# One-core attention and mixture-of-experts kernel: the next image's Layer 0 from turn 12 on, sorting in every other turn beside expert tiles, and a reordered tail

## The chip, the cores and the metric

The kernel runs on one core of one Trainium2 chip, as one program in one launch. Its time is the device time of a whole execution in microseconds; the median of several executions is compared. Everything is float32.

## The reference

The input x has 8 images of 256 channels by 32x32 pixels, that is 1024 tokens of 256 values each. Three stages follow each other for every image, and images do not mix.

```python
# Layer 0: deformable attention with a learned position bias
x = x + L0(_gn(x))          # L0: q = wq x; a 6x6 depthwise convolution (stride 4), gelu, 1x1, tanh -> 64 offsets;
                            # sample x there -> k, v (64 keys); for each query and key an MLP of the signed-log
                            # distance gives the bias: relu(relu(pos w1) w2) w3;  softmax(q k + bias) v ; w_out
# Layer 1a: sigmoid attention over the 1024 tokens of the image
t = t + sigmoid(LN(t) qw LN(t)^T) LN(t)
# Layer 1b: mixture of experts, top 2 of 8
t = t + moe(LN(t))          # moe: u + sum over the two chosen e of weight_e * (gelu(u w1[e]) w2[e] + b2[e])
```

The position bias is the bulk of the work: for each image a two-layer network of width 64 over 1024 queries x 64 keys x 4 heads.

## The kernel before

**The turn.** The program is unrolled. Its main loop runs 8 images x 64 turns (`for n in range(NB * TURNS)`, `b, i = divmod(n, TURNS)`). Each turn makes two tiles of the bias network. `first_layer` writes one tile `h` on DVE (L463) and one on POOL (L465), two turns ahead of use. `second_layer` multiplies two tiles on PE (`h2p`, L478) and rectifies one on ACT (L484) and one on DVE (L486). In even turns `third_layer` adds four finished tiles to the logits (`sim`, L505). The PSUM pool of `h2p` has two buffers, so the second product of a turn cannot start before L486 of the turn before has emptied its buffer.

**What is laid beside it.** All other work is written as Python generators, and each turn advances some of them by one step, so that the order on every engine is the order of the calls. At the end `in_order` fixes it: every engine carries out its instructions in the order in which the program issued them. In one turn the calls come in this order: the bias tiles, `side.step()`, `advance(mains)`, `mix(b, i)`, `step(sums)`.

- `side` holds the softmaxes of the logits (`waiting`) and `prep`, Layer 0 of the next image: statistics, normalization, two projections (`qs`, L272), the 36 taps of the convolution on DVE (L284, L286, three a step), gelu, the offset projection (`op`, L297), tanh, positions (`gk`, `ft`), sampling weights `wt` (ACT L377 and L379, POOL L368), transposes (`tp`, L374), and keys and values (`kv` L386, `kp`, `kd`).
- `mains` holds `attention`, in two halves. `upper` runs in turns 53 to 63 of its own image, `rest` in the next image's turns 0 and on: `to_query` (5 to 11), the attention `slots` (12 to 28), the normalization `finish` (to 33), the sort `route`, and 16 indirect DMAs on POOL (L775) that send the tokens to the rows of their experts in DRAM.
- `route` is six steps on DVE with little else: two picks of the best expert, running counts, the count product `cnt` on PE (L842), the slots (`slot`), and which expert owns each tile (`which`, `expert`). It keeps the one bank of the PSUM pool `acc` from its first step to its last. `cnt` is taken in its fourth step and read to the end in the fifth, in one of the two buffers of the pool `psum`.
- `mixtures` holds `experts` of the image two before: 12 tiles of 256 rows (15 single-expert tiles for the last image). One step stores tile n-2 (`yp` L921, `yt` L926, `ys`), computes tile n-1 (`hp` L939, `ht` L947), and loads and transposes tile n (`xl` L900, `tp` L957, `xg` L959). Weights are fetched through SP, with the expert's number read from `expert` (L906, L907).
- `sums` holds `combine` of the image three before: gathers `gs` on POOL (L992), a weighted sum on DVE (`xc`, L984), transposes and stores.

While `attending` is set, `aside` takes its bank from `psum`, else from `acc`. While `sorting` is set, `side` starts no softmax step and no step of `prep`. So in the loop the sort stands alone in turns 34 to 39, the sends follow in turns 40 to 55, and `mix` has no tile due in turns 35, 37 and 39. Image 0 has no `rest`, images 0 and 1 have no tiles, and image 7 has no `prep`.

**The tail.** After the loop, `rest` of the last image goes on, with one step of `mixtures` (image 6) after every second step until the sort has begun, and after every step from there on. Then the last image's experts and sums alternate.

Of the kernel before, what the change touches and what calls it, by code (L numbers as in the profile page):

```python
# [16 lines left out]
P = 128  # L17
# [86 lines left out]
def tile_conv_attn_hybrid(ctx: ExitStack, tc: tile.TileContext, x, par, qw, w1, w2_, cst, out):  # L104
# [32 lines left out]


    attending = sorting = False

    def aside(name):
        return psum(name) if attending else acc(name)
# [72 lines left out]
    def run(steps):  # L215
        for _ in steps:
            pass
# [374 lines left out]


    def attention(b, st, o, rt):
        nonlocal attending
        x = xres.pop(b)
        x1, tt, tn, qt = None, None, None, None

# [148 lines left out]
        def rest():  # L747
            nonlocal attending, sorting, ut, lqs
            for n, _ in enumerate(softmax(st, 1, 1, st["last"], o, psum)):
                if n == 1:  # L750
                    residual_bias(1)
                yield
            yield from to_query(1)
            ut = tokens("ut")
            lqs = low("lqs", (P, Q))
            attending = True

            for n, _ in enumerate(slots([(q, mp) for q in range(4) for mp in range(2 if q < 2 else 0, 4)], True)):
                if n % 3 == 0:
                    yield  # L760
                    others()
                yield
                others()
            attending = False
            while finishing:
                yield
                others()
            attending = sorting = True
            yield from route(lqs, rt, LARGE if b == NB - 1 else SMALL)
            attending = sorting = False  # L770

            xs, group = xss[b % 2], f"slots{b}"
            for n in range(16):
                m, c = divmod(n, 2)
                sent = nc.gpsimd.indirect_dma_start(  # L775
                    out=xs[:, :], out_offset=bass.IndirectOffsetOnAxis(ap=rt["slot"][:, c, m : m + 1], axis=0),
                    in_=ut[:, m, :], in_offset=None,
                )
                if n:
                    tc.declare_no_dep(sent.ins, group=group, reason="other slots")  # L780
                tc.add_to_no_dep_group(group, sent.ins)
                sents.add(sent.ins.name)
                yield
            rt.update(xs=xs, xu=xu)
            mixtures.append((b, experts(b, rt)))
# [6 lines left out]
    def route(lqs, rt, slots_):  # L792
# [74 lines left out]
            nc.vector.tensor_reduce(place[:, c], part(1), AX.X, ALU.add)  # L867
        slot = held("slot", (P, 2, 8), I32)
        nc.vector.tensor_copy(slot, place)  # L869
        yield  # L870
        which = bank[:, 0 : TILES * (E - 1)].rearrange("p (t e) -> p t e", e=E - 1)
        nc.vector.tensor_tensor(
            which, ends[:, 1:8].unsqueeze(1).to_broadcast([P, TILES, E - 1]),
            cst_("tiles").unsqueeze(2).to_broadcast([P, TILES, E - 1]), ALU.is_le,
# [2 lines left out]
        nc.vector.tensor_reduce(whose, which, AX.X, ALU.add)  # L877
        expert = held("expert", (P, TILES), I32)
        nc.vector.tensor_copy(expert, whose)
        yield  # L880
        rt.update(slot=slot, expert=expert, w=ws)

# [1 line left out]
    def experts(b, rt):  # L886
        xs = rt["xs"]
        slots_ = LARGE if b == NB - 1 else SMALL

        several = LARGE // slots_  # L890
        rounds = -(-tiles_of(slots_) // several)
        yv = dram.tile([rounds * LARGE, C], F32, name=f"ys{slots_}")
        rows, tokens_, first, second = {}, {}, {}, {}

        def at(t):
            return slice(t * LARGE, (t + 1) * LARGE)

        def fetch(t):
            rows[t] = low("xl")
            nc.sync.dma_start(out=rows[t], in_=xs[at(t), :].rearrange("(s p) c -> p s c", p=P))  # L900

        def weights(t, pool, width, w, name):
            f = pool.tile([P, 2, width], F32, name=name)
            for u in range(several):
                n = t * several + u
                e = nc.sync.value_load(rt["expert"][0:1, n : n + 1], min_val=0, max_val=E - 1)  # L906
                nc.sync.dma_start(out=f[:, u, :], in_=w[bass.ds(e, 1)].rearrange("e p c -> (e p) c"))  # L907
            return f

        fetch(0)  # L910
        yield
        fetch(1)
        first[0] = weights(0, w1pool, 2 * C + 2, w1, "w1")
        yield
        for n in range(rounds + 2):
            if n >= 2:
                f2, ht = second.pop(n - 2), tokens_.pop(n - 2)
                yp = psum("yp").rearrange("p (s c) -> p s c", s=2)
                for s in range(2):
                    for f in range(2):  # L920
                        nc.tensor.matmul(  # L921
                            yp[:, s, :], lhsT=ht[:, f, s * P : (s + 1) * P],
                            rhs=f2[:, s * several // 2, f * C : (f + 1) * C], start=(f == 0), stop=(f == 1),
                        )
                yt = low("yt")
                nc.vector.tensor_tensor(yt, yp, f2[:, 0:several, 2 * C :].to_broadcast([P, 2, C]), ALU.add)  # L926
                nc.sync.dma_start(out=yv[at(n - 2), :].rearrange("(s p) c -> p s c", p=P), in_=yt)
            if n + 2 < rounds:
                fetch(n + 2)
            if n < rounds:  # L930
                second[n] = weights(n, w2pool, 3 * C, w2_, "w2")
            if 1 <= n <= rounds:
                f1, xg = first.pop(n - 1), tokens_[n - 1]
                hp = psum("hp").rearrange("p (f i) -> p f i", f=2)
                for f in range(2):
                    for u in range(several):
                        us = slice(u * slots_, (u + 1) * slots_)
                        for k in range(2):
                            nc.tensor.matmul(  # L939
                                hp[:, f, us], lhsT=f1[:, u, k * C + f * P : k * C + (f + 1) * P], rhs=xg[:, k, us],  # L940
                                start=(k == 0), stop=(k == 1),
                            )
                tokens_[n - 1] = ht = low("ht")
                for f in range(2):
                    for u in range(several):
                        us = slice(u * slots_, (u + 1) * slots_)
                        nc.scalar.activation(  # L947
                            ht[:, f, us], hp[:, f, us], AF.Gelu, bias=f1[:, u, 2 * C + f : 2 * C + f + 1]
                        )
            if n + 1 < rounds:  # L950
                first[n + 1] = weights(n + 1, w1pool, 2 * C + 2, w1, "w1")
            if n < rounds:
                xl = rows.pop(n)
                tp = aside("tp").rearrange("p (k i) -> p k i", k=2)
                for k in range(2):
                    for s in range(2):
                        nc.tensor.transpose(tp[:, k, s * P : (s + 1) * P], xl[:, s, k * P : (k + 1) * P], ident)  # L957
                tokens_[n] = xg = low("xg")
                nc.scalar.copy(xg, tp)  # L959
            if n < rounds + 1:  # L960
                yield
        sums.append((b, combine(b, rt, yv)))
# [35 lines left out]
    class Side:  # L998
# [2 lines left out]
        def __init__(self, prep_steps):  # L1001
            self.prep, self.waiting, self.busy, self.left = prep_steps, [], True, True

        def step(self):
            busy = False
            if self.waiting and not (sorting and self.busy):
                busy = self.busy
                self.busy = next(self.waiting[0], None)
                if self.busy is None:
                    self.waiting.pop(0)  # L1010
                    self.busy = True
            if self.left and not busy and not sorting:
                self.left = next(self.prep, self) is not self

        def finish(self):
# [49 lines left out]
    def mix(b, i):  # L1065
        of = mixtures[0][0] if mixtures else NB
        if of == b - 2 and b < NB - 1:
            due = i in (24, 26) or i > 26 and i % 2 and i not in (35, 37, 39, 59, 61, 63)
        elif of == b - 3:
            due = i == 9  # L1070
        else:
            due = b == NB - 1 and (i >= TURNS - 2 if of == b - 1 else of < b and i > 9 and (i % 2 or i % 3 == 0))
        if due:
            step(mixtures)
# [4 lines left out]

    for n in range(NB * TURNS):  # L1080
        b, i = divmod(n, TURNS)
        if i == 0:
            steps = iter(())
            if b + 1 < NB:
                xb = big("xb")
                nc.sync.dma_start(out=xb, in_=xin(b + 1))
                steps = prep(b + 1, xb, sts[b + 1])
            side = Side(steps)
# [21 lines left out]
        if coming_ < total:  # L1110
            if n % 8 == 3:
                scale()
            elif n % 8 == 4:
                second()
        if i > 4:
            side.step()
        if ready:
            side.waiting.append(ready)
        if i == 0 and b:
# [11 lines left out]
    n = sorted_ = 0  # L1131
    while mains:
        advance(mains)
        if sorted_ or not attending and n % 2:
            step(mixtures)
        sorted_ = sorted_ or sorting
        n += 1
    while mixtures:
        step(mixtures)
# [111 lines left out]
```

## Time and profile before

| what | value |
|---|---|
| median of 3 runs | 3132.17 us (3131.75 to 3134.66) |
| the profiled execution, its own time | 3125.55 us |
| its span, first to last instruction | 3123.8 us |
| PE busy | 2832.1 us (91%), mean granted clock 0.975 |
| DVE busy | 2170.5 us (69%) |
| ACT, POOL busy | 1824.4 us (58%), 1558.2 us (50%) |
| main loop (turn 0 of image 0 to turn 63 of image 7) | 72.9 to 2867.0 us |
| one image in the loop, images 2 to 6 | 358.3, 363.8, 362.3, 364.5, 362.4 us |

The start of a turn is told by the ACT instruction of `second_layer` (L484), of which there is one in each turn; the 512 of them cut the span into turns of 2.4 to 12 us. Idle time of PE inside a turn is what that turn has lost, as long as PE has the most work there. Where DVE has more, PE's idle time shows DVE's excess. The profiled execution is 6.6 us shorter than the median of the runs.

### The profile page before, as it was taken

What the parts mean: (1) busy time and instruction counts of PE and PEld (TensorE: products, weight loads), DVE (VectorE), ACT (ScalarE), POOL (GpSimd) and SP (SyncE); (2) the same over time, 40 slices, a digit from 0 to 9 for tenths busy, and PEclk for the clock granted to TensorE, in tenths of its full rate; (3) what the DMA queues carried; (4) which work ended last, traced back from release to release, by engine and by line L of the source; (5) the groups of instructions that cost most, each with busy time, mean ns of one, the idle gap of its engine ahead of it and who ended that gap; (6) DMA issues with size and microseconds to landing.
All of it is one profiled execution on the core that took longest, in us unless ns stands there. A gap on an engine that the chain in (4) does not pass through costs nothing. (4 is left out here: it accounts for less than half of the span.)

```text
span 3123.8 us, 51635 instructions
## 1 busy us (share of the span) xinstructions
PE 2832.1 (91%) x19592; PEld 1395.6 (45%) x19592; DVE 2170.5 (69%) x2999; ACT 1824.4 (58%) x2533; POOL 1558.2 (50%) x945
## 2 busy tenths in 40 slices
PE   3888998899999999999999999899999999979975
PEld 2223343233545344453545445354444545514764
DVE  4897678967776687857876678766877574595122
ACT  3666565665576566665566656665666666554322
POOL 2546454744455364645556455553646443383122
PEclk7999999999999999999999999999999999989998
DMA  3312101211256125531346223561245325631386
GB/s 106 83 32 48 21 14 32 58 38 21 75 139 187 23 63 140 168 107 43 77 111 208 51 57 100 144 179 33 61 132 173 88 78 153 173 97 57 112 280 221
DMA packets 428297, 311.21 MB, mean 100 GB/s; under 512 B 284432, under 2 KB 368656, under 8 KB 428048
## 3 DMA queue, kind: packets, MB, share of 16 engines
q1 hardware_dynamic: 415472, 273.14, 32.7%
q0 software_dynamic: 12288, 33.57, 3.4%
q8 instruction: 154, 2.52, 0.3%
q10 hardware_dynamic: 288, 1.20, 0.1%
q14 instruction: 95, 0.78, 0.1%
HBM read 239.93 MB, written 67.90 MB: 99 GB/s over the span
## 5 line engine op out<-in xcount | busy, mean ns | idle before, releaser
L465 POOL TENSOR_TENSOR h<-ta,nb 128x1024 f32<-128x1024 f32 x512 | 1071.6, 2095 | 1036.2 <-PE h2p L478 913.1
L478 PE MATMUL h2p<-h,pr__100 64*64 64x512 f32 x8192 | 1028.3, 610 | 131.8 <-DVE h L486 107.5
L486 DVE TENSOR_TENSOR h<-h2p,nc 128x1024 f32<-128x1024 f32 x512 | 624.6, 1220 | 461.4 <-PE h2p L478 454.7
L484 ACT ACTIVATE h<-h2p,pr__100 128x1024 f32<-128x1024 f32 x512 | 570.9, 1115 | 517.0 <-PE h2p L478 515.8
L463 DVE TENSOR_TENSOR h<-ta,nb 128x1024 f32<-128x1024 f32 x512 | 769.2, 1503 | 0.3
L470 ACT ACTIVATE h<-h 128x1024 f32<-128x1024 f32 x512 | 538.0, 1051 | 63.4 <-POOL h L465 63.2
L478 PEld LDWEIGHTS h2p<-h,pr__100 64*64 64x64 f32 x8192 | 253.7, 133 | 658.0 <-issue 295.1
L505 PE MATMUL sim<-h,pr__100 128*32 128x512 f32 x4096 | 511.5, 618 | 0.0
L505 PEld LDWEIGHTS sim<-h,pr__100 128*32 128x32 f32 x4096 | 109.5, 112 | 377.8 <-issue 377.8
L713 PE MATMUL ap<-qt,tn 128*128 128x256 f32 x1024 | 250.5, 388 | 0.5 <-ACT nc L451 0.5
L727 PE MATMUL vp<-tt,sg 128*128 128x256 f32 x1024 | 243.3, 381 | 0.3 <-ACT sg L718 0.3
L992 POOL DMA_INDIRECT gs<-ys,slot x128 | 139.0, 1086 | 175.3 <-DMA ys<-yt 55.7
L713 PEld LDWEIGHTS ap<-qt,tn 128*128 128x128 f32 x1024 | 185.2, 190 | 88.5 <-issue 55.0
L947 ACT ACTIVATE ht<-hp,w 128x128 f32<-128x128 f32 (+1 forms) x366 | 108.6, 377 | 196.8 <-PE hp L939 173.2
L921 PE MATMUL yp<-w,ht 128*128 128x256 f32 x792 | 196.2, 390 | 13.7 <-DMA w<-in_w 7.0
L727 PEld LDWEIGHTS vp<-tt,sg 128*128 128x128 f32 x1024 | 193.2, 190 | 33.2 <-issue 6.9
L939 PE MATMUL hp<-xg,w 128*128 128x128 f32 (+1 forms) x1464 | 197.0, 287 | 6.7 <-ACT gk L307 2.8
L939 PEld LDWEIGHTS hp<-xg,w 128*128 128x128 f32 x1464 | 187.8, 194 | 18.3 <-ACT gk L307 3.7
L775 POOL DMA_INDIRECT xs<-ut,slot x128 | 167.8, 1311 | 51.0 <-DVE slot L869 29.4
L921 PEld LDWEIGHTS yp<-w,ht 128*128 128x128 f32 x792 | 144.4, 191 | 73.0 <-issue 34.0
L926 DVE TENSOR_TENSOR yt<-yp,w 128x512 f32<-128x512 f32 x99 | 68.3, 690 | 153.5 <-PE yp L921 127.3
L286 DVE SCALAR_TENSOR_TENSOR oc<-qp,pr__100,oc 128x128 f32<-128x128 f32 x280 | 168.9, 603 | 7.2
(266 smaller groups left out, 2468.0 us busy)
## 6 DMA issues: line engine op xcount, KB each, us to landing
w<-in_w SPq DMA_DIRECT2D x183, 384.0 KB, 3.6
w<-in_w SPq DMA_DIRECT2D x183, 257.0 KB, 3.7
ta<-fd SPq DMA_DIRECT2D x128, 256.0 KB, 5.5
xl<-xs SPq DMA_DIRECT2D x99, 256.0 KB, 3.7
ys<-yt SPq DMA_DIRECT2D x99, 256.0 KB, 2.3
nb<-fd SPq DMA_DIRECT2D x128, 128.0 KB, 5.3
xb<-in_x SPq DMA_DIRECT2D x8, 1024.0 KB, 7.2
x<-in_x SPq DMA_DIRECT2D x8, 1024.0 KB
```

Source lines behind the costliest of these rows:

```text
L286: nc.vector.scalar_tensor_tensor(oc, tap, dw[:, t : t + 1], oc, ALU.mult, ALU.add)
L463: nc.vector.tensor_tensor(h1, a, b, ALU.max)
L465: nc.gpsimd.tensor_tensor(h1, a, b, ALU.subtract)
L470: nc.scalar.activation(h1, h1, AF.Relu)
L478: nc.tensor.matmul(h2p[gs, r, :], lhsT=par_("w2")[rs, gs], rhs=h1[rs, g].rearrange("p y x -> p (y x)"), start=True, stop=True, tile_positi ...
L484: nc.scalar.activation(h2, h2p, AF.Relu, bias=par_("cb2"))
L486: nc.vector.tensor_tensor(h2.rearrange("p r (y x) -> p r y x", x=W), h2p.rearrange("p r (y x) -> p r y x", x=W), nc_.unsqueeze(3).to_broad ...
L505: nc.tensor.matmul(sim[32 * q : 32 * q + 32, :], lhsT=par_("z3")[:, 15 - m : 47 - m], rhs=h2s[2 * u + q // 2][:, q % 2, :], start=False, s ...
L713: nc.tensor.matmul(ap[:, u, :], lhsT=tn[:, k, m0 : m0 + P], rhs=qt[:, k, quarter(q)], start=(k == 0), stop=(k == 1),)
L727: nc.tensor.matmul(vp[:, i, :], lhsT=sg_[:, u, i * P : (i + 1) * P], rhs=tt[:, 2 * mp + u, :], start=(first and u == 0 and i == 0), stop=( ...
L921: nc.tensor.matmul(yp[:, s, :], lhsT=ht[:, f, s * P : (s + 1) * P], rhs=f2[:, s * several // 2, f * C : (f + 1) * C], start=(f == 0), stop ...
L939: nc.tensor.matmul(hp[:, f, us], lhsT=f1[:, u, k * C + f * P : k * C + (f + 1) * P], rhs=xg[:, k, us], start=(k == 0), stop=(k == 1),)
```

## The change

Four things move; no arithmetic is added or removed.

1. `prep` may start in turn 12 instead of turn 5 (image 0 excepted), and no longer stops for the sort.
2. In the loop, the first five steps of the sort are taken in odd turns only, 35 to 43. In the even turns between them `side` goes on; in the odd ones it doesn't. The sixth step (`which`, `expert`) moves behind the second send, in turn 45, and `which` is written to SBUF instead of to the PSUM bank. The sends fall in turns 44 to 59 instead of 40 to 55.
3. Tiles of `experts` are due in turns 24 and 26, and in the odd turns 31 to 55. Before they were due in 24 and 26, 27, 29, 31, 33, and in the odd turns 41 to 57. So each of the sort's five odd turns now holds a step of `experts` too.
4. In the tail, tiles come after every second step of the sort, not after each; and the first tile's `w1` is requested ahead of its tokens (everywhere, in the loop too).

```diff
@@ attention, rest
-            yield from route(lqs, rt, LARGE if b == NB - 1 else SMALL)
+
+            steps = route(lqs, rt, LARGE if b == NB - 1 else SMALL)
+            for _ in range(5):
+                while b < NB - 1 and turn % 2 == 0:
+                    yield
+                next(steps)
+                yield
             attending = sorting = False
...
                 sents.add(sent.ins.name)
+                if n == 1:
+                    run(steps)
                 yield
@@ route
         nc.vector.tensor_copy(slot, place)
-        yield
-        which = bank[:, 0 : TILES * (E - 1)].rearrange("p (t e) -> p t e", e=E - 1)
+        rt.update(slot=slot, w=ws)
+        yield
+        which = one.tile([P, TILES, E - 1], F32, name="which")
...
         nc.vector.tensor_copy(expert, whose)
-        yield
-        rt.update(slot=slot, expert=expert, w=ws)
+        rt.update(expert=expert)
@@ experts
+        first[0] = weights(0, w1pool, 2 * C + 2, w1, "w1")
         fetch(0)
         yield
         fetch(1)
-        first[0] = weights(0, w1pool, 2 * C + 2, w1, "w1")
         yield
@@ Side
-        def step(self):
+        def step(self, both=True):
...
-            if self.left and not busy and not sorting:
+            if self.left and both and not busy:
@@ mix
-            due = i in (24, 26) or i > 26 and i % 2 and i not in (35, 37, 39, 59, 61, 63)
+            due = i in (24, 26) or 30 < i < 56 and i % 2
@@ main loop
+        turn = i
...
-        if i > 4:
-            side.step()
+        if i > 4 and not (sorting and i % 2):
+            side.step(i > (11 if b else 4))
@@ tail
-        if sorted_ or not attending and n % 2:
+        sorted_ = sorted_ or sorting
+        if n % 2 if sorting else sorted_ or not attending and n % 2:
             step(mixtures)
-        sorted_ = sorted_ or sorting
```

What that does to the turns of an image with tiles (2 to 6), in the order of the program:

| work | turns before | turns after |
|---|---|---|
| `prep`: statistics and normalization | 5 to 11 | 12 to 20 |
| `prep`: `qs` projections | 12, 13 | 21, 22 |
| `prep`: 36 taps, three a step | 14 to 27 | 23 to 32, 34, 36 |
| `prep`: gelu, `op`, positions | 28 to 34 | 38 to 47 |
| `prep`: `wt`, `tp`, then `kv`, `kp` | 43 to 48, then 50, 52 | 50 to 56, then 57, 58 |
| sort, five steps | 34 to 38 | 35, 37, 39, 41, 43 |
| sort, sixth step | 39 | 45 |
| sends | 40 to 55 | 44 to 59 |

More of the change, by code (lines that the diff above doesn't have):

```diff
@@ L139, in tile_conv_attn_hybrid @@
     attending = sorting = False
+    turn = 0
     def aside(name):
@@ L594, in attention @@
     def attention(b, st, o, rt):
-        nonlocal attending
         x = xres.pop(b)
```

## The prediction

> **What bounds the kernel now.** I read the page first, then where PE waits within one steady image, then the stretches with idle time, then the instructions in them.
>
> ```profile
> span 3123.8 us, 51635 instructions
> PE 2832.1 (91%) x19592; PEld 1395.6 (45%) x19592; DVE 2170.5 (69%) x2999; ACT 1824.4 (58%) x2533; POOL 1558.2 (50%) x945
> PE   3888998899999999999999999899999999979975
> ```
>
> PE is the bound almost everywhere; only the start and the last slices are thin. A reordering can win idle time of PE and nothing else: about 280 us, of which 190 lie in the loop. Here are the longest waits of PE in image 4 (1404.1 to 1766.4 us):
>
> ```profile
> PE h2p L478 <- DVE h L486: 8.8, 7, 2.0
> PE q L649 <- ACT tn L642: 1.8, 1, 1.8
> ```
>
> Image 4 loses 16.9 us in all, and half of it is PE waiting for DVE to empty the PSUM buffer of the bias product. The busy times of stretches show where (first three rows: turns 6 to 8, 28 to 33 and 34 to 41 of image 4; last row: turns 28 to 49 of image 1, which has no expert tiles):
>
> ```profile
> core 0: us, PE busy (x) PEld busy (x) DVE busy (x) ACT busy (x) POOL busy (x), PEclk, DMA share, GB/s
> 1438.38:1450.74 12.36, 10.26 (x88) 2.70 (x84) 11.26 (x24) 6.17 (x7) 6.18 (x5) 1.00 0.08 12
> 1566.42:1601.82 35.40, 34.04 (x270) 18.59 (x266) 21.84 (x35) 25.35 (x43) 16.73 (x9) 1.00 0.53 133
> 1601.82:1639.77 37.95, 31.67 (x241) 10.74 (x237) 33.60 (x59) 22.99 (x29) 20.87 (x11) 0.96 0.31 78
> ...
> 505.33:609.50 104.17, 84.60 (x644) 24.73 (x640) 94.80 (x118) 66.82 (x86) 67.55 (x39) 0.95 0.21 48
> ```
>
> In rows 1, 3 and 4 DVE has more work than PE, and PE's idle time is that excess. In row 2 PE has far more. The third row is the sort: 6.3 us idle. One of its stalls in the timeline:
>
> ```profile
> 1608.31 2.63 DVE L463 TENSOR_TENSOR h<-ta,nb 128x1024 f32<-128x1024 f32 x1
> 1610.86 1.21 DVE L486 TENSOR_TENSOR h<-h2p,nc 128x1024 f32<-128x1024 f32 x1
> ...
> 1612.12 1.57 PE L478 MATMUL h2p<-h,pr__100 64*64 64x512 f32 x8 [1.97 <-DVE h L486]
> ```
>
> The sort's ops delay L463, L463 delays L486, and PE stands 1.97 us. L463 takes 1.22 us where nothing is in its way, here 2.63.
>
> [...] L463 (1.22 or 2.63 us) and the tap L286 (0.45 us in the timeline, 0.603 in the mean, up to 2.0) have two SBUF inputs, L486 reads PSUM and stays at 1.2. So a DVE-bound stretch is longer than its bare sums. [...] The trace has clock 0.96 in the sort's row; its 1.57 us for 8 products of L478, against 1.09 elsewhere, is such a phase. Image 5 has the same stalls without it and isn't shorter, so I give it no gain. [...] the request of `w1` goes out at 3015.19, behind the two fetches of tokens that waited until 3013.46.
>
> **The change, part by part.** PE's work is the same, so each part is idle time of PE, for one image of 2 to 6 unless said.
>
> *Prep leaves turns 5 to 11.* DVE loses four L243 (0.68 us), two L244 (0.21), and the small statistics (0.75 together), some 3.9 us in turns 5 to 7, PE two products (0.8). The 2.0 us stall of turn 8 goes: image 7, which has no prep, doesn't have it. The stall of 1.8 us at `q` stays: POOL's L465 stands there behind a gather that waits for the last `ys`, and that order is untouched. In turns 12 and 13 PE loses `qs` (4 us) while DVE gains the statistics; DVE then has 10.3 us for PE's 8.5, turns 11 and 14 are PE's and cover most: -0.2. Part: **+1.8**.
>
> *Tiles leave turns 27 to 33, taps enter.* PE loses two and a half tile steps (yp 1.99, hp 1.95, tp 0.60, so 4.5 us each) and gets fewer `op` products: 34.0 - 10 = 24 us. DVE loses two yt (0.69) and the position ops (3.0), and gains five groups of taps: at 0.603 us 9.0, so 21.8 - 4.4 + 9.0 = 26.5[...]. The row turns from PE-bound to DVE-bound. Following the L463, L486 and h2p of each turn from row to row I get stalls of 2 us in turns 31 and 32 and 4.0 in all. Bounds: bare taps at 0.45 leave 1.9[...]. The 1.36 us that PE loses in turn 29 today (waits for ACT there) go. Part: **-2.6** (-5.3 to -0.5).
>
> *Sort beside tiles.* The odd turns 35, 37, 39 get a tile step (4.5 us of PE) next to 1.4 to 2.4 us of sort on DVE, and turns 41 and 43 keep theirs. PE then has 6.5 to 8 us in an odd turn, DVE 5 to 6: the 6.3 us of turns 34 to 41 are covered. What is late next: in turn 41 `cnt` takes one of the two `psum` buffers until turn 43, and `attending` sends `tp` there too, so yp, hp and tp go through the other one by one. hp waits for yt (0.7 to 1.5 us), tp for four ht (1.14 us and a start). The tail shows such a step today (hp waited for yt, below). I take 2.5 us, and 1.0 for the softmax, `which` and yt that meet in turn 45: DVE has some 8 us there, PE 7 and a free turn after it. Sends, `wt` and L465 on POOL make 4.7 us of a turn of 6 to 8 in turns 53 to 56. Part: 6.3 - 3.5 = **+2.8** (0 to 4.5).
>
> Moved `kv`, `kp`, position ops: they lie in turns where PE has its own work, and the next image reads them in its turn 2, 44 turns' work of slack shrunk to 8. SP's nine small loads move from 34 to 47; the bias terms that read them are asked for in turn 56. `w1` ahead of the tokens in turn 24: the sends landed long before, nobody waits on SP. Each of these: nothing; if the cover were gone, the 2 us of one stall.
>
> Sum for an image of 2 to 6: +1.8 - 2.6 + 2.8 = +2.0; five images **+10**.
>
> *Image 1* is DVE-bound in turns 28 to 49 (94.8 of 104.2 us). Seven groups of taps enter (bare 9.4 us). PE's 5.5 us wait in turn 31 for the blocking chain gelu, tanh, log goes, since its steps now have a turn between them; so do 2 us of turn 8 and some 2 in turns 57 and 58, filled by `kv`. Net **-2** (-6 to +3). *Image 7*: same DVE sum, spread wider, DVE-bound still: 0. *Image 0*: untouched.
>
> *Tail.* Today:
>
> ```profile
> 2986.44 0.69 DVE L926 TENSOR_TENSOR yt<-yp,w 128x512 f32<-128x512 f32 x1 [2.26 <-PE yp L921]
> 2987.19 3.78 PE L939 MATMUL hp<-xg,w 128*128 128x128 f32 x16 [0.78 <-DVE yt L926]
> 2988.82 1.03 POOL L775 DMA_INDIRECT xs<-ut,slot  x1 [26.98 <-DVE slot L869]
> ...
> 3013.46 0.87 SPq L900 DMA_DIRECT2D xl<-xs  x2
> 3015.19 0.36 SPq L907 DMA_DIRECT2D w<-in_w  x1
> ```
>
> The sort lies 2972.6 to 2988.5 with three tiles in it. With one tile less ahead of the slots, they come some 6 us sooner, and the 16 sends (1.27 us apart) end at about 3003 in place of 3008.9. But the tokens can be fetched only behind the last `ys` of image 6 on SP, whose yt ran at 3011.7, and these tiles wait for weights; so most of the 6 us is hidden. `w1` is asked for some 2 us sooner and hp no longer waits 1.4 for it. **+3** (0 to +7).
>
> Total 10 - 2 + 3 = **11 us**. The profiled execution becomes 3125.6 - 11 = 3114.6; the median shown lies 6.6 above its time: 3132.2 - 11 = **3121**.
>
> **Rivals.** *Slower: the taps' turns decide.* Place: turns 28 to 33 of images 1 to 6. Price: L463 at 2.4 us (its slow mode in the trace) in place of 1.22 in each turn is +1.2 x 6 = 7 us an image; half hidden, 3.5 to 4.5 more than I booked, six times: 11 - 25 = -14, 3146. It is slower as soon as the stretch costs 2.9 us an image more than my 4.0 ((11 + 6.3)/6). For it: row 4 has DVE at 91%. Against it: PE has some 18 us of work in turns 33 to 35, behind which DVE catches up. *No change: the idle time only moves.* The bank of turn 41 takes 4.5 us in place of 2.5 and the tail gives nothing: 11 - 10 - 3 = -2, 3134. For it: DVE's total falls by nothing. *The full gain*: the taps' stall stays at its lower bound and the cold clock of the sort goes too: 11 + 5 x 2.1 + 3 = 24, 3108. Against it: cold phases were hidden before.
>
> **How the numbers follow.** A difference of about 0.2% (6.3 us) can be told from none. Forecast with its better variant 0.60, idle time moves 0.20, taps decide 0.20. Faster below 3125.9: 0.60; within 0.2%: 0.21; slower above 3138.4: 0.19. The range runs from the full gain with 4 us of unknown to most of the slower case: 3104 to 3143.
>
> **What would show it.** Right: no stall in turn 8; PE above 95% in turns 34 to 45, with one hp waiting for yt and one tp for ht in turn 41; PE idle 3 to 5 us in turns 28 to 33; sends ending near 3003 before the shift; loop images 2 us shorter. Wrong: turns 28 to 33 losing over 7 us, or L465 and the sends delaying ACT L470 in turns 56 to 59.

## The result, and the profile after

The changed kernel is slower: 3200.63 us median of 4 runs (3194.78 to 3206.0), beside 3131.96 (3130.93 to 3134.66) for the kernel before in the same session; ratio 1.0216, with a 95% interval of 1.0202 to 1.023 (so in all brackets behind ratios below). Forecast were 3121 us and a gain of 11. The medians differ by 69 us. The two profiled executions differ by 80, since the one before (3125.55 us) was shorter than its median and the one after (3206.0) longer; the account below is of these 80. Line numbers of the bias network and of `prep` are one higher than before (L463 is L464), those of `experts` eight higher (L926 is L934); those of the attention in between (L649) are the same.

The page after: span, busy times, PE's busy tenths, and two groups, that of PE's product h2p and that of the taps (busy us, mean ns, idle before and its releaser):

```profile
span 3204.2 us, 51597 instructions
PE 2855.9 (89%) x19592; PEld 1395.7 (44%) x19592; DVE 2117.2 (66%) x2999; ACT 1828.5 (57%) x2534; POOL 1528.9 (48%) x945
PE   3888998889899998999989999899989999978976
L479 PE MATMUL h2p<-h,pr__100 64*64 64x512 f32 x8192 | 1037.0, 616 | 156.7 <-DVE h L487 132.2
L287 DVE SCALAR_TENSOR_TENSOR oc<-qp,pr__100,oc 128x128 f32<-128x128 f32 x280 | 174.6, 623 | 7.2
```

The 80 us have two parts. PE's gaps, from its first matmul on, add up to 335.1 us where they were 278.7: +56. And the same 19,592 matmuls are busy for 23.8 us longer: they ran at half clock more often (phases with a granted clock of 0.50 add up to 95.6 us in images 1 to 6, before to 34.1). DVE is busy for 53 us less than before (2170.5), so DVE's total tells nothing here; *when* it is busy does.

PE's longest waits in image 4 (1446.12 to 1822.54 us; us in total, times, longest):

```profile
PE h2p L479 <- DVE h L487: 10.6, 5, 6.2
PE cp L447 <- DVE yt L934: 2.3, 1, 2.3
PE q L649 <- ACT tn L642: 2.1, 1, 2.1
```

Before, the first was 8.8 us in seven waits of at most 2.0. Now there is one of 6.2, and a new one at `cp`. Next, the busy times of turns 6 to 8, 28 to 33 and 34 to 41 of image 4, and of turns 28 to 49 of image 1:

```profile
core 0: us, PE busy (x) PEld busy (x) DVE busy (x) ACT busy (x) POOL busy (x), PEclk, DMA share, GB/s
1480.37:1490.28 9.91, 9.47 (x84) 2.28 (x80) 8.62 (x16) 6.18 (x7) 6.82 (x5) 1.00 0.09 16
1609.10:1646.00 36.90, 27.64 (x208) 10.34 (x204) 31.91 (x42) 18.80 (x26) 15.49 (x9) 0.91 0.42 115
1646.00:1691.13 45.13, 43.09 (x334) 23.19 (x330) 28.81 (x50) 28.77 (x46) 15.67 (x8) 1.00 0.57 165
509.37:616.36 106.99, 82.27 (x609) 22.66 (x605) 96.39 (x133) 57.77 (x68) 56.35 (x31) 0.90 0.14 36
```

In row 1, the stall of turn 8 is gone. In row 3, the sort is covered: PE is busy for 43.1 of 45.1 us. In row 2, PE has 62 matmuls fewer than before (208 for 270), and yet the stretch became 1.5 us longer; PE stands idle for 9.3 us of it, and the mean clock is 0.91. The timeline of its turns 30 to 32 (start, us, instruction, idle before it and the releaser):

```profile
1620.12 1.68 POOL L580 TENSOR_TENSOR lrs<-lrs,power 128x2 f32<-128x2 f32 x1 [2.50 <-DVE lsh L578]
1622.03 5.74 POOL L466 TENSOR_TENSOR h<-ta,nb 128x1024 f32<-128x1024 f32 x3
1622.28 5.65 DVE L287 SCALAR_TENSOR_TENSOR oc<-qp,pr__100,oc 128x128 f32<-128x128 f32 x3
...
1627.86 2.27 DVE L464 TENSOR_TENSOR h<-ta,nb 128x1024 f32<-128x1024 f32 x1
1630.05 1.21 DVE L487 TENSOR_TENSOR h<-h2p,nc 128x1024 f32<-128x1024 f32 x1
1631.18 1.39 DVE L287 SCALAR_TENSOR_TENSOR oc<-qp,pr__100,oc 128x128 f32<-128x128 f32 x3
1631.31 1.98 PE L479 MATMUL h2p<-h,pr__100 64*64 64x512 f32 x8 [6.20 <-DVE h L487]
...
1633.23 3.14 PE L506 MATMUL sim<-h,pr__100 128*32 128x512 f32 x16
```

Read it from the bottom. PE waits 6.20 us for L487. L487 is short but stands in DVE's queue behind three taps that took **5.65 us** and an L464 of 2.27. Three taps alone take 1.39 (at 1631.18). The 5.65 are as long as the three subtractions that GpSimd ran back to back beside them, 5.74 us from 1622.03. Ahead of them GpSimd had stood 2.50 us for the statistics and then had the `pow` to do, while PE went through turns of 2.5 and 3.7 us that have no tile in them; so three subtractions were due at once. After the stall PE works at half clock (granted clock 0.50 from 1628.90 to 1635.73): 8 products in 1.98 us (1.09 at full clock), 16 of `sim` in 3.14 (1.93 at full clock).

PE's idle time of one image, mean of images 2 to 6, by the steps of the prediction:

| step | turns | before, us | after, us | won | forecast |
|---|---|---|---|---|---|
| prep leaves 5 to 11 | 7 to 22 | 4.8 | 3.9 | +0.9 | +1.8 |
| tiles leave 27 to 33, taps enter | 29 to 33 | 1.2 | 9.4 | -8.2 | -2.6 |
| sort beside tiles | 34 to 45 | 6.7 | 2.8 | +3.9 | +2.8 |
| kv, kp, c loads later | 47 to 60 | 1.4 | 6.5 | -5.1 | 0 |
| all turns | | 17.2 | 25.6 | -8.5 | +2.0 |

With the half clock such an image is 12.5 us longer (374.8 for 362.3). Image 1 is 11.4 longer: the chain gelu, tanh, log no longer stalls it (5.98 us in turn 31 became 1.25), but turn 32 now stalls 6.93, turn 38 4.52 and turn 60 5.76. Image 7 idles 3.8 us more than before and image 0 1.7 us more. The tail became 256.0 us in place of 256.8.

### The profile page after: what moved, and what is told of

The parts are those of the page before. It is cut to its first block, busy times and chain, and to the rows that moved or that the text cites. A ratio compares the mean times of both kernels' runs of the same rounds, so it can differ in the third digit from the quotient of the medians.

```text
span 3204.2 us, 51597 instructions
## 1 busy us (share of the span) xinstructions
PE 2855.9 (89%) x19592; PEld 1395.7 (44%) x19592; DVE 2117.2 (66%) x2999; ACT 1828.5 (57%) x2534; POOL 1528.9 (48%) x945
## 5 line engine op out<-in xcount | busy, mean ns | idle before, releaser
L487 DVE TENSOR_TENSOR h<-h2p,nc 128x1024 f32<-128x1024 f32 x512 | 624.6, 1220 | 595.4 <-PE h2p L479 590.6
L464 DVE TENSOR_TENSOR h<-ta,nb 128x1024 f32<-128x1024 f32 x512 | 710.0, 1387 | 0.3
L781 POOL DMA_INDIRECT xs<-ut,slot x128 | 154.5, 1207 | 63.8 <-DVE slot L877 35.2
L934 DVE TENSOR_TENSOR yt<-yp,w 128x512 f32<-128x512 f32 x99 | 68.2, 689 | 154.0 <-PE yp L929 131.2
## 6 DMA issues: line engine op xcount, KB each, us to landing
ta<-fd SPq DMA_DIRECT2D x128, 256.0 KB
xl<-xs SPq DMA_DIRECT2D x99, 256.0 KB
ys<-yt SPq DMA_DIRECT2D x99, 256.0 KB
```

What stands on the lines that cost most here:

```text
L464: nc.vector.tensor_tensor(h1, a, b, ALU.max)
L487: nc.vector.tensor_tensor(h2.rearrange("p r (y x) -> p r y x", x=W), h2p.rearrange("p r (y x) -> p r y x", x=W), nc_.unsqueeze(3).to_broad ...
```

## The experiments

Each kernel was compared with runs of the kernel before on the same chip beside it, whose medians were 3133 to 3146 us; so ratios are compared here, and times only within a profile. "Idle" is PE's idle time in an image, mean of images 2 to 6.

**1. Prep from turn 5 again, the rest of the change kept.**

```
-            side.step(i > (11 if b else 4))
+            side.step()
```

> The changed kernel with prep started in turn 5 again (sort in odd turns, tile schedule and tail stay). Theory taps (the convolution's taps in turns 28 to 32 meet finish, and its PE stall of 1.2 + 6.2 + 1.8 us in turns 31 to 33, with the half-clock phase behind it, is most of the 10 to 14 us that every image lost): the stall is gone, six images gain about 10 us each, 3140 us or less. Rival sort (the sort beside tiles, with one psum buffer held by cnt, is what costs): at most 20 us gained, 3180 or more.

Ratio 1.0045 (1.0032 to 1.0058), idle 19.5 us. About four fifths of the loss go, so the late start of prep is part of it. The stretch of 28 to 33 is still short of PE work: without tiles in 27 and 29 the chain gelu, tanh, log of prep shows as 3.0 us in turn 31. Neither theory's number was met: what is left lies between them.

**2. The kernel before with prep from turn 12 in images 1 to 6, nothing else.**

```
-            side.step()
+            side.step(i > (11 if b else 4))
```

> The kernel before with one part of the change alone: prep may start only in turn 12 (image 0 excepted), still pausing during the sort. Theory taps: taps lie in turns 28 to 32 as in the changed kernel, but the tile steps of turns 29, 31, 33 still stand there and give PE some 10 us of work that hides the stall in images 2 to 6; image 1, without tiles, stalls some 7 us. 3135 to 3160 us. Rival sort: this part is harmless or a gain, 3120 to 3132.

Ratio 0.999 (0.9977 to 1.0003), idle 16.9 us, and turns 31 to 33 lose 0.4. The number is the rival's: taken as a ratio, the late start of prep alone does no harm. The places are the theory's: in images 2 to 6 the same taps in the same turns cost nothing while the tiles are still there, and in image 1, which has no tiles, turn 32 stalls 6.9 us. So it isn't the taps by themselves.

**3. The kernel before with the tail's part of the change alone** (tiles in every other turn of the tail's sort, `w1` ahead of the tokens).

> The kernel before with the tail's order and the request of w1 ahead of the tokens alone. Both theories: the stretch after the loop was 256.8 us before and 256.0 after, so within 3 us of the kernel before. If the tail matters, 5 us or more either way.

Ratio 1.0009 (1.0001 to 1.0018); the tail has 265.1 us, as in experiment 2 with the old tail in the same session. The part gains nothing; it doesn't explain the loss either.

**4. The changed kernel, in turns 24 to 33 with prep's step behind `advance`** instead of ahead of it, so that the statistics that GpSimd waits for come ahead of the taps.

```
-        if i > 4 and not (sorting and i % 2):
+        late = 23 < i < 34
+        if not late and i > 4 and not (sorting and i % 2):
...
         advance(mains)
+        if late:
+            side.step(i > (11 if b else 4))
```

> The changed kernel with side.step (the taps) issued behind advance (finish's statistics) in turns 24 to 33, so that DVE does the statistics first and POOL's factors are released about 1.7 us sooner; the same instructions in the same turns. Theory lock (POOL waits for the late statistics in turn 30, then runs three L466 back to back[...]): the burst falls apart, the 6.2 us stall of turn 32 falls below 3, total 3170 to 3185 us. Rival sum (DVE simply has more work there than PE, whatever the order): the stalls of turns 31 to 33 keep their sum within 1.5 us, total 3193 to 3206.

Ratio 1.0192 (1.0174 to 1.0211). Turns 30 to 33 stall 2.3, 0.6, 3.1 and 2.3 us, 8.3 in all for 9.3: the stall is cut up, but its sum stays, as the rival said. The order of these two steps isn't the cause. The slowdown only moved: the taps of turns 28 to 33 take 10.0 us for 11.2, two of the L464 2.88 us each, and DVE is busy for 31.2 us of the stretch (31.9 in the changed kernel).

**5. The changed kernel with the old turns for the tiles.**

```
-            due = i in (24, 26) or 30 < i < 56 and i % 2
+            due = i in (24, 26) or i > 26 and i % 2 and i not in (35, 37, 39, 59, 61, 63)
```

> The changed kernel with the old turns for the expert tiles (24, 26, odd ones from 27 but 35, 37, 39). Theory 'no cover': turns 28 to 33 lose time because two tile steps of 4.5 us of TensorE work left them while the taps came; with the tiles back the stall in turns 30 to 33 falls from 9.3 us to under 1.5 an image, the half clock behind it goes, and the time is 1.000 to 1.007 of the kernel before (turns 34 to 41 may lose some 3 us again, since the sort has turns without a tile, and the late kv and kp keep their 4 us). Rival 'late work': the loss is the late kv, kp and sort beside tiles, so it stays above 1.012.

Ratio 1.0154 (1.0123 to 1.0186): a miss for the theory, and above the rival's 1.012. Turns 31 to 33 behaved as the theory said (0.4 us for 9.3). But turn 38 opened:

```profile
1642.92 4.41 DVE L287 SCALAR_TENSOR_TENSOR oc<-qp,pr__100,oc 128x128 f32<-128x128 f32 x3
...
1647.25 1.21 DVE L464 TENSOR_TENSOR h<-ta,nb 128x1024 f32<-128x1024 f32 x1
...
1648.38 1.21 DVE L487 TENSOR_TENSOR h<-h2p,nc 128x1024 f32<-128x1024 f32 x1
...
1649.52 0.22 DVE L835 SCALAR_TENSOR_TENSOR lp<-oh,lp 128x64 f32<-128x64 f32 x1
1649.65 1.48 PE L479 MATMUL h2p<-h,pr__100 64*64 64x512 f32 x8 [4.57 <-DVE h L487]
...
1651.06 3.17 PE L506 MATMUL sim<-h,pr__100 128*32 128x512 f32 x16
```

The taps of turn 36 now stand where no tile is: the kernel before halts prep during the sort; this one doesn't. They take 4.41 us beside GpSimd's subtractions, and L464 and L487 stand behind them. The sort's ops of turn 37 (L835 and on) come on DVE only after this stall. So it is the same stall as in turn 32, in another place without tiles. The sort itself is a second lump of DVE work: where it stood alone, in turns 34 to 41 of the kernel before, PE lost 6.7 us. Each of the two needs tiles beside it. Half clock follows this stall too: 8 products take 1.48 us for 1.09, 16 of `sim` 3.17 for 1.93.

**6. The changed kernel with its thirteen tile steps in the odd turns 27 to 51.**

```
-            due = i in (24, 26) or 30 < i < 56 and i % 2
+            due = i in (24, 26) or 26 < i < 52 and i % 2
```

> The changed kernel with its thirteen tile steps in the odd turns 27 to 51 in place of 31 to 55: tiles beside the taps and beside the sort. Theory 'no cover': the stall in turns 30 to 33 falls to under 1.5 us, the sort keeps its cover (turns 34 to 41 lose some 2 us), only the late kv and kp still cost 4 us in turns 47 to 60, perhaps more as turns 53 and 55 now have no tile; an image loses 13 to 16 us idle and the time is 0.997 to 1.003 of the kernel before. Rival 'late work': above 1.01.

Ratio 1.0052 (1.0028 to 1.0076), idle 17.9 us. Turns 28 to 33 and 34 to 41:

```profile
1576.53:1611.00 34.47, 32.94 (x260) 17.44 (x256) 28.30 (x43) 21.58 (x36) 15.85 (x9) 1.00 0.49 133
1611.00:1656.17 45.17, 43.12 (x334) 23.19 (x330) 28.86 (x50) 28.99 (x46) 15.69 (x8) 1.00 0.69 202
```

One edit of the list of turns takes three quarters of the loss away. The first stretch now does 52 matmuls more than in the changed kernel in 2.4 us less, though DVE has still 28.3 us there. Idle time and ratio are each a little above the range expected; the turns meant are right (0.4 us in 31 to 33, 2.0 in 34 to 41), the late work costs more than I had allowed.

**7. The changed kernel, but in turns 28 to 33 GpSimd fills `h1` with zeros** and reads nothing; the subtraction is left out there.

```
+        if of and 27 < turn < 34:
+            nc.gpsimd.memset(h1, 0.0)
+            return h1, None
         nc.gpsimd.tensor_tensor(h1, a, b, ALU.subtract)
```

> The changed kernel, but in turns 28 to 33 of images 1 to 7 GpSimd fills h1 with zeros (no input from SBUF) where it subtracts; the subtraction is left out there. [...] three taps take some 1.5 us in every turn, not up to 5.7, the stall in turns 30 to 33 falls from 9.3 us to under 3, and the time is 1.003 to 1.010 of the kernel before. Rival 'DVE's own sum': DVE's work alone is longer than TensorE's there; the stall stays at 6 us or more and the time at 1.015 or above.

Ratio 1.0063 (1.0041 to 1.0085), inside the first of the two ranges: where GpSimd reads nothing, the taps aren't slow. The same place in the timeline:

```profile
1598.63 1.84 POOL L467 MEMSET h<- 128x1024 f32 x2
1598.90 1.42 DVE L287 SCALAR_TENSOR_TENSOR oc<-qp,pr__100,oc 128x128 f32<-128x128 f32 x3
```

Beside two fills the three taps take 1.42 us; beside three subtractions they took 5.65. The stretch of image 4 has 30.3 us for 36.9, at full clock, and DVE is busy for 26.5 us of it, not 31.9. Turns 31 to 33 still stall 4.6 us (expected under 3), 2.8 of them in turn 33, where a group of taps stands beside the first real subtraction again and takes 2.83 us. So about half of the stall goes with the reads; the rest stays where PE, without its tiles, has 25.6 us of work beside DVE's 26.5. A fill is also quicker than a subtraction (0.95 for 1.91 us), so part of the gain may be that `h1` was ready sooner; the taps' 1.42 us lie within the time of the two fills (1598.63 to 1600.47).

**8. The changed kernel without the taps of turns 28 to 32** (15 of 36 taps of each prepared image are left out).

```
-                nc.vector.scalar_tensor_tensor(oc, tap, dw[:, t : t + 1], oc, ALU.mult, ALU.add)
+                if not 27 < turn < 33:
+                    nc.vector.scalar_tensor_tensor(oc, tap, dw[:, t : t + 1], oc, ALU.mult, ALU.add)
```

> The changed kernel with the five groups of taps of turns 28 to 32 left out (15 of 36 taps of each prepared image; turns without their tiles stay as they are). Both theories on the stretch: the stall of 9.3 us falls to under 1.5 and the half clock behind it goes; what stays is what the late kv and kp cost, and the time is 0.997 to 1.005 of the kernel before. If it stays above 1.01, the taps are not what the turns lack.

Ratio 0.9978 (0.9967 to 0.999), idle 17.0 us, turns 29 to 33 lose 1.0. With these taps gone, turns without tiles are harmless. Everything else in the change together is worth at most these 7 us; forecast for it were 5 x (1.8 + 2.8) = 23, less 2 in image 1, and 3 in the tail. The 15 taps less flatter it.

**9. The changed kernel with the eight loads of `c` from `fd` asked for one step of prep later.**

The wait at `cp` in turn 52 hangs on `nb`, whose load stands in turn 48 of the program. SP's own waits in 1700 to 1752 us of the changed kernel, and the timeline:

```profile
SPq L350 <- DMA fd<-ft: 6.8, 1, 6.8
```

```profile
1717.48 0.43 SPq L1064 DMA_DIRECT2D x<-in_x  x1
1719.66 0.33 SPq L341 DMA_DIRECT2D fd<-ft  x1
1726.86 3.59 SPq L350 DMA_DIRECT2D c<-fd  x8
...
1740.91 0.73 SPq L437 DMA_DIRECT2D nb<-fd  x1
...
1745.70 1.87 DVE L441 TENSOR_SCALAR nb<-nb,pr__100 128x512 f32<-128x512 f32 x1 [4.38 <-DMA nb<-fd]
...
1750.21 0.55 PE L447 MATMUL cp<-nb,pr__100 64*64 64x128 f32 x8 [2.30 <-DVE yt L934]
```

SP stands for 6.8 us until `fd` has landed, and the `ys`, the weights and the bias loads of turn 48 queue up behind it. The edit moves the eight loads behind the next `yield` of prep, into turn 48.

> The changed kernel with the eight loads of c from fd asked for one step of prep later (turn 48, behind the bias loads of that turn; before them in turn 47). Theory 'SP stands for fd': SP waits 6.8 us for fd to land before these loads, so the ys, the weights and the bias loads of turn 48 go out late, DVE waits 4.4 us for nb and TensorE 2.5 us in turn 52; here the wait of SP goes, the stall in turn 52 falls from 2.5 us to under 0.8 in images 1 to 6, and the time is 0.003 to 0.006 below the changed kernel's ratio of 1.0216, so 1.015 to 1.019. Rival 'DVE is busy anyway' (yt waits behind the softmax): turn 52 keeps 1.5 us or more and the ratio stays at 1.019 to 1.024.

Ratio 1.0161 (1.0146 to 1.0176), and turn 52 stalls 0.68 us for 2.48 in the mean of images 2 to 6, as before the change; in image 1 it keeps its 2.7 us. In this kernel nothing waits for `nb` any longer:

```profile
1728.19 0.48 DVE L441 TENSOR_SCALAR nb<-nb,pr__100 128x512 f32<-128x512 f32 x1
...
1734.79 0.45 PE L447 MATMUL cp<-nb,pr__100 64*64 64x128 f32 x8
```

So 1.8 of the 5.1 us of late work are this wait on SP's queue. The step in the ratio, 0.0055 or 17 us, is more than five such waits: in the changed kernel half-clock phases followed the wait in turn 52 in three images, and PE's busy time falls by 10 us (2845.7 for 2855.9).

The 6.8 us aren't the landing of `fd` alone. Two microseconds ahead of it, in the same turn, SP asks for the 1 MB of the next image's `x` (L1064). In the kernel before, where the store of `fd` comes some 60 us ahead of that load in image 4, SP waited 1.7 us for it:

```profile
SPq L349 <- DMA fd<-ft: 1.7, 1, 1.7
```

And in image 1 of the changed kernel, where `x` was asked for 45 us earlier, the loads of `c` go out 1.6 us behind the request of `fd`; in images 2 to 6 it is 4.7 to 7.2. That the load of `x` delays `fd` is read from these times; no run moves that load.

**10. Experiment 6 with prep from turn 9 in images 2 to 6, and from 5 in image 1.**

```
-            side.step(i > (11 if b else 4))
+            side.step(i > (8 if b > 1 else 4))
```

> The changed kernel with the tile steps in the odd turns 27 to 51 and prep from turn 9 on in images 2 to 6 (from 5 in image 1). Theory: the taps of turns 27 to 31 stand beside tiles, the sort has its tiles, fd, kv and kp come three to five turns sooner; image 1 is back at the 32 us idle that it had with prep from 5, images 2 to 6 lose 12 to 15 us in place of 17.2 before, and the time is 0.991 to 0.997 of the kernel before. Rival 'what is won is given back': the sort's turns from 34 on carry prep's statistics chain as well, idle time stays at 17 us or more, 0.998 to 1.006.

Ratio **0.9967** (0.9954 to 0.998): faster than both kernels. The page's busy times, and PE's longest wait in image 4:

```profile
span 3134.4 us, 51672 instructions
PE 2831.5 (90%) x19592; PEld 1396.0 (45%) x19592; DVE 2124.8 (68%) x2999; ACT 1835.1 (59%) x2538; POOL 1550.3 (49%) x945
```

```profile
PE h2p L479 <- DVE h L487: 5.3, 4, 2.1
```

PE is busy for 24 us less than in the changed kernel, at a mean granted clock of 0.975 for 0.966. Idle is 16.7 us, more than expected: turns 31 to 40 lose 0.5 and turn 52 0.7, but turns 57 to 60 lose 4.9: no tile and no `kv` lies there any more.

**11. The kernel before with prep from turn 9 in images 2 to 6.**

> The kernel before with nothing changed but the start of prep in images 2 to 6: turn 9 in place of 5. Theory: the stall of 2 us in turn 8 goes, tiles stay beside the taps, kv and kp move by four turns and cost nothing; 1.5 to 2 us an image, 0.996 to 0.999 of the kernel before. Rival 'late work costs': kv and kp behind turn 54 cost as much as turn 8 gives, 0.9985 to 1.002.

Ratio 0.9994 (0.9986 to 1.0002). Turn 8 gives 1.97 us; turns 7, 13, 37, 38 and 53 take 2.9 more than before, and idle is 17.8 us. Alone it is no gain. In its profile, of the same session as that of experiment 10, turns 34 to 41 lose 7.4 us for 2.1 there, turns 57 to 60 0.7 for 4.9, and PE is busy for 3.3 us more. That experiment 10 gains by the sort beside tiles is read from these turns, not tested by itself.

**12. Experiment 10 with the tile steps of turns 47 and 49 moved to turns 55 and 57.**

```
-            due = i in (24, 26) or 26 < i < 52 and i % 2
+            due = i in (24, 26) or 26 < i < 58 and i % 2 and i not in (47, 49, 53)
```

> The kernel of the run before last (prep from turn 9, tile steps in the odd turns 27 to 51), but with the tile steps of turns 47 and 49 and one more (53 was free already) moved: odd turns 27 to 45, 51, 55 and 57. Theory 'cover': the 4.9 us that TensorE waits in turns 57 to 60, where only the statistics chain on DVE runs, fall to under 2, turns 47 and 49 lose at most 1 us since TensorE has transposes of prep there; 0.990 to 0.996 of the kernel before. Rival 'moved, not saved': turns 47 to 50 lose what turns 57 to 60 win, 0.996 to 1.000.

Ratio 0.9983 (0.9976 to 0.999), the rival's number. Turns 57 to 60 lose 0.7 us for 4.9, but turn 49 takes 0.7 and turn 52 2.8. Idle falls to 15.4 us, and the kernel isn't faster for it: the stalls moved, and its profile has 3.2 us more of busy PE than experiment 10 (2834.7). Its interval touches that of experiment 10, so which of the two is better stays open; both beat the kernel before.

## Why the prediction was wrong

**Right: what bounds the kernel, and where.** No stall in turn 8; PE above 95% in the sort's turns; in turn 41 one `hp` waiting for `yt` and one `tp` for `ht`, 2.0 us where 2.5 were booked:

```profile
1686.05 2.05 PE L947 MATMUL hp<-xg,w 128*128 128x128 f32 x16 [0.78 <-DVE yt L934]
...
1689.33 0.66 PE L965 MATMUL tp<-cs,xl 128*128 128x128 f32 x4 [1.23 <-ACT ht L955]
```

The sort's part came out better than forecast (+3.9 for +2.8), prep's somewhat worse (+0.9 for +1.8, since small waits came in turns 7, 13 and 21 to 22).

**Wrong, the step that failed: "Tiles leave turns 27 to 33, taps enter".** It forecast a stall of 4.0 us, at most 6.7; 9.3 were measured, over the 7 us that the prediction had named as a sign of being wrong. The direction was seen (the row turns DVE-bound), and the place: turns 31 and 32. Mis-sized was what DVE's ops pay beside GpSimd's subtractions. I gave the taps their mean over the whole kernel, 0.603 us, and took the upper bound from the 0.8 us a turn by which DVE's ops exceeded their shortest times in turns 28 to 49 of image 1 before (16.9 us in 22 turns). DVE's work was to be 26.5 us and is 31.9: the fifteen taps take 11.2 us for the 9.0 booked, and two of the six L464 take 2.27 and 2.88 us in place of 1.22, which makes 2.7. In turns 31 and 32 GpSimd's subtractions come without a gap, and there a tap takes 1.8 to 1.9 us, about as long as the subtraction beside it (1.9 to 2.0). Without GpSimd's reads (experiment 7) DVE's work is the 26.5 us of the forecast, and the stall is 4.6 us, close to its 4.0. With the tiles back (experiment 6) DVE is busy for 28.3 us of the stretch in image 4, not 31.9, and its L464 at 1592.47 and 1597.10 us take 1.22 us each. So what failed is the price of the slowdown in turns that have lost their tiles. The slowdown itself is shown by the runs: three taps take 5.65 us beside three subtractions of 5.74, and 1.42 beside fills that read nothing. The mean over 280 taps hardly shows it (603 ns before, 623 after), and L464's even fell (1503 to 1387 ns). A stretch that becomes bound by another engine can't be costed with means over stretches in which that engine had slack.

My rival "the taps' turns decide" named this place and this slowdown, with 3.5 to 4.5 us an image more than booked and a chance of 0.20; it took 5.3 more. It priced the slowdown by an L463 of 2.4 us in every turn, called its slow mode; but before the change L463 took anything from 1.2 to 4.1 us, and in the stretch two of six were slow, and the taps of one turn. The objection to it, that PE's work in turns 33 to 35 gives DVE time, didn't hold: a wait of PE that has happened isn't won back where PE is the bound afterwards.

**Wrong: "so I give it no gain", of the half-clock phases.** They were put at nothing because image 5 has the same stalls without the phase and isn't shorter than image 4. But image 5 also has 3.0 us more idle time (19.9 for 16.9), so the comparison couldn't show what a phase costs. In the changed kernel the stall of turn 32 (6.2 us, 6.9 in image 1) had a phase of 6.83 us at a granted clock of 0.50 in each of the images 1 to 6. Before the change stalls of 2.0 us had one of 3.41 us at 0.50, in some images (in turn 36 of all of 1 to 6 but 5); so how long a stall has to be isn't shown. The longer busy time that goes with the phases is 23.8 us of the 80.

**Wrong: "Each of these: nothing".** The late `kv`, `kp` and `c` loads cost 5.1 us an image. 1.8 of it is shown: SP waits for `fd` in turn 47, right behind the load of `x`, where it waited in turn 34. I had asked who reads the nine loads, and not what stands on SP ahead of `fd` and behind the wait for it. Another 1.5 us show in turn 60, after DVE has run its four `c` ops (2.63 us in image 4, beside a subtraction) ahead of L464; turns 47 and 53 take 0.9 each. These three were read from the trace and not tested one by one.

**Wrong, smaller: images 1 and 7, and the tail.** Image 1 was to lose 2 us and lost 11.4: turns 32 and 38 stall behind slow taps and L464, turn 60 behind the late work. Image 7 was put at 0 and idles 3.8 us more; that was not followed up. The tail gained 0.8 us, not 3. The slots did come 6 us sooner in it, as forecast, and hardly anything came of it: experiment 3.

The sum of idle time: +10 us was forecast for images 2 to 6, and -42 measured; for image 1 -2, and -8 measured. With images 0 and 7 it is about -56, and the clock's 24 come on top.

## What to carry to other kernels

Where one engine's instructions last longer beside another's, as the taps did here (5.65 us for 1.39), cost a stretch with the longer durations as soon as filler work leaves it, and ask in which turns the other engine will run without gaps. Work that looks like load on the bound engine may be the cover of another: spread it to every stretch where the second engine has a lump, and don't trade one lump's cover for another's. When a transfer that waits for data is moved, list what its queue holds ahead of it and behind it at the new place.

## What the runs showed of the hardware

- Three taps beside three back-to-back subtractions of GpSimd (5.74 us) took 5.65 us, alone 1.39, and beside two fills of the same tile (1.84 us), which read nothing from SBUF, 1.42.
- In images 1 to 6 of the changed kernel each half-clock phase (granted clock 0.50) lasted 3.41 or 6.83 us. Each of the eight stalls of 4.5 us or more had one of 6.83. Behind stalls of 1.8 to 3.4 us there was one of 3.41 in some images and none in others with the same stall, and once one of 6.83.
- From the request of the store of `fd` to the first load that reads it back, SP took 4.7 to 7.2 us in images 2 to 6 of the changed kernel, where a 1 MB load had been asked for some 2 us ahead of the store, and 1.6 us in image 1, where that load was 45 us older. Before the change, with the load behind the store, it was 1.6 to 3.5 us.
